# Class tokens' atom products on three column groups, ahead of the patches' first product

## The chip, the cores and the metric

The kernel runs on one core of a Trainium2 chip. Its time is the device time of one execution, in microseconds; it is given as the median of several runs. TensorE (PE) multiplies, with its weight loads shown as PEld; VectorE (DVE), ScalarE (ACT) and GpSimd (POOL) do the elementwise work; SyncE (SP) issues the transfers from HBM. Each engine executes its own instructions in order.

## What is computed

The program is a network of four layers on 512 tokens of width 768. The change lies in the feed-forward part of the second layer (`L1_ffn`). Of its 512 tokens the first six are class tokens, the others patches:

```python
patch_out = gelu(patch_tokens @ fc1_w.T + fc1_b) @ fc2_w.T + fc2_b          # hidden width 192
gate_logits = einsum('bnd,nrd->bnr', l2norm(cls_tokens), l2norm(gate_pair)) + balance_bias
route_probs = softmax(gate_logits); chosen_route = argmax(route_probs)
hid_all = gelu(einsum('bnd,ahd->bnah', cls_tokens, atom_in_w) + atom_in_b)  # 5 atoms x 192
sh_pair = hid_all[:, arange(6)[:, None], src, :]
route_candidates = einsum('bnrh,nrdh->bnrd', sh_pair, atom_out_w[dst]) + atom_out_b[dst]
cls_out = candidate of the chosen route * its probability
return concatenate([cls_out, patch_out], axis=1)
```

Each class token is a row of 768 numbers. It goes through one product to 5 x 192 = 960 hidden numbers (atom-in), is routed, and goes through a second product from 960 back to 768 (atom-out). All of it is in fp32.

## The kernel before

Tokens lie in four tiles of 128 partitions; `xfT` is the normalized input with features on the partitions, in six chunks of 128. The kernel is written with a framework that decides the order of the instructions on each engine when the program is built: it follows the text of the kernel, but moves instructions ahead where it expects them to be ready earlier. Waits between engines come from the use of tiles.

Around the change stand these steps, with their lines:

- L1600: the last product of the graph layer, into `x`. Behind each tile, `Norm` (L230 to L254) takes statistics on VectorE, the square root on ScalarE (L245), and writes the normalized tile `xf` on ScalarE (L254).
- L274: PE transposes `xf` into PSUM; ScalarE (L205) and VectorE (L207) copy it to `xfT` in turn. The transposes of the first two tiles come before those of the last two.
- L298 and L1625: the patches' first product (`fc1`) and its Gelu, into `hid`.
- L1639 to L1667: the routing of the class tokens, on VectorE with a square root (L1641) and an exponential (L1654) on ScalarE; ends with `coef`, the share of each atom for each destination, and `cb`.
- L1677 and L1678: atom-in, in two halves of 480 columns; six matmuls each, with six tokens as the stationary operand, all into the same PSUM partitions; then the bias. L1679 is the Gelu.
- L1685 and L1687: the hidden rows mixed by `coef` into `hin`; L1692 to L1697 transpose them into `hT` (96 partitions, ten chunks of six tokens) and `cb` into `cbT`.
- L1704 to L1706: atom-out, in two halves of 384 columns; ten matmuls with `hT` and one with `cbT` (the bias) each.
- L308: `token_product`, here the patches' second product (`fc2`), whose results are added to `x` (L318), with the statistics of the next norm behind them.

Two helpers matter. `weights` (L143 to L149) takes the next of three weight buffers in turn (`w_tile`) and issues one transfer on SyncE's queue; a transfer waits until what used the buffer three turns before is done, and what stands behind it in the queue waits too. One of the buffers serves until L1600 as `room` for the edges of the graph layer. `routed` (L358 to L375) is the router of other layers: it puts six matmuls on three groups of 32 columns of the array by writing to PSUM partitions 0 to 31, 32 to 63 and 64 to 95; ScalarE copies the 96 rows, and a matmul with the constant `three` (three stacked identities of eight columns) adds the three groups up. `ready` loads a weight and lets POOL make differences of its quarters (L438 to L441); the next layer's first weight, `L2_gnn_W`, is the next that does so.

Of the kernel before, what the change touches and what calls it, by code (L numbers as in the profile page):

```python
# [10 lines left out]
FP = mybir.dt.float32  # L11
# [3 lines left out]
AF = mybir.ActivationFunctionType  # L15
# [3 lines left out]
P = 128  # L19
N = 512  # L20
D = 768
NT = N // P
KC = D // P
HC = D // 2
# [3 lines left out]
HD = 64  # L28
# [69 lines left out]
def kernel(ctx: ExitStack, tc: tile.TileContext, a: dict, out: bass.AP):  # L98
    nc = tc.nc
    V, S, G, T = nc.vector, nc.scalar, nc.gpsimd, nc.tensor  # L100
# [20 lines left out]
    def w_tile(name="w", held=None):  # L121
        pool, n = turn_ = turns.pop(0)
        (turns if held is None else held).append(turn_)
        return pool.tile([P, KC * D], FP, tag="w" + n, name=name)

    def psum():
        return psp.tile([P, 512], FP, tag="ps", name="ps")
# [7 lines left out]
    def feature_major(name):  # L135
        return big_tile(name)[:, : KC * N].rearrange("p (k n) -> p k n", k=KC)
# [6 lines left out]
    def weights(src, p=P):  # L143

        k, n = src.shape[0] // p, src.shape[1]
        w = w_tile()
        v = w[:, : k * n].rearrange("p (k n) -> p k n", k=k)
        nc.sync.dma_start(v[:p], src.rearrange("(k p) n -> p k n", p=p))
        return v  # L149
# [9 lines left out]
    def spread(src, offset, n, parts=P):  # L159

        return bass.AP(tensor=src.tensor, offset=src.offset + offset, ap=[[0, parts], [1, n]])

    def row_tile(name, n=D):
        return rowp.tile([P, KC * (P + 2)], FP, tag="row", name=name)[:, :n]
# [12 lines left out]
    def col(name, i=0, p=P):  # L177
        c = _COL_AT[name] + i
        return cols[:p, c : c + 1]
# [113 lines left out]
    def feature_product(w, xT, f, width=P):  # L293

        ps = psum()
        n = xT.shape[1]
        for k in range(n):
            T.matmul(ps[:width], w[:, k, f : f + width], xT[:, k, :], start=k == 0, stop=k == n - 1)  # L298
        return ps[:width]
# [47 lines left out]
    G3 = 3 * 32  # L347
    three = const.tile([P, 8], FP, name="three")
# [3 lines left out]
    def router_weights(w_dram, e):  # L352
        w = small.tile([P, KC, 32], FP, tag="rt_w", name="rt_w", bufs=1)
        G.memset(w, 0.0)
        nc.sync.dma_start(w[:, :, :e], w_dram.rearrange("(k p) e -> p k e", p=P))
        return w

    def routed(w, xT, e, use):  # L358

# [535 lines left out]
    with tc.tile_pool(name="gat0", bufs=2) as gp:  # L895
# [46 lines left out]
        for i in range(9):  # L942
# [10 lines left out]
            if i < 8:  # L953
                h, s4, d4 = heads(i) if i else head0
# [183 lines left out]
    xfT, xs, rest = n.T, n.split, n.rest  # L1138
    with tc.tile_pool(name="ffn0", bufs=2) as fp:
# [113 lines left out]
        w2a, w2b = sw[:, KC * 384 : KC * 384 + D], sw[:HD, KC * 384 + D : KC * 384 + 2 * D]  # L1253
# [119 lines left out]
    HW = 96  # L1373
# [240 lines left out]
    with tc.tile_pool(name="ffn1", bufs=1) as fp:  # L1614
        NCLS, NA, H = 6, 5, 192
        C = NCLS
        big1 = token_major("cls1")[:C]
        cls = big1[:, 1, :]
        G.tensor_copy(cls, x[:C, 0, :])
        add_row_to(x, row("f1_b2"))  # L1620
        w1 = weights(a["L1_ffn_fc1_w"])
        hid = feature_major("hid")
        for f, width in ((0, P), (1, HD)):
            ps = feature_product(w1, xfT, f * P, width)
            S.activation(hid[:width, f, :], ps, AF.Gelu, bias=col("f1_b1", f, width))  # L1625


        big2 = token_major("cls2")[:C]
        gpair = big1[:, 2:, :]
        nc.sync.dma_start(gpair, a["L1_ffn_gate_pair"])  # L1630
        bal = fp.tile([C, 2], FP, name="bal")
        nc.sync.dma_start(bal, a["L1_ffn_balance_bias"])
        route = fp.tile([C, 2, NA * NA], FP, name="route")
        nc.sync.dma_start(route, a["route"])
        ss = fp.tile([C, 3], FP, name="ss")
        junk, unit = big2[:, 3, :], big2[:, :3, :]
        rows3 = [xf[:C, 0, :], gpair[:, 0, :], gpair[:, 1, :]]
        for i, v in enumerate(rows3):
            V.scalar_tensor_tensor(junk, v, 1.0, v, op0=ALU.mult, op1=ALU.mult,  # L1639
                                   accum_out=ss[:, i : i + 1])  # L1640
        S.activation(ss, ss, AF.Sqrt)  # L1641
        V.tensor_scalar(ss, ss, 1e-12, None, op0=ALU.max)
        V.reciprocal(ss, ss)
        for i, v in enumerate(rows3):
            V.tensor_scalar(unit[:, i, :], v, ss[:, i : i + 1], None, op0=ALU.mult)
        lo = fp.tile([C, 2], FP, name="lo")
        for i in range(2):
            V.scalar_tensor_tensor(junk, unit[:, 0, :], 1.0, unit[:, i + 1, :], op0=ALU.mult,
                                   op1=ALU.mult, accum_out=lo[:, i : i + 1])
        V.tensor_add(lo, lo, bal)  # L1650
        mx = fp.tile([C, 4], FP, name="mx")
        V.tensor_reduce(mx[:, 0:1], lo, AX.X, ALU.max)
        V.tensor_scalar(lo, lo, mx[:, 0:1], None, op0=ALU.subtract)
        S.activation(lo, lo, AF.Exp)  # L1654
        V.tensor_reduce(mx[:, 1:2], lo, AX.X, ALU.add)
        V.reciprocal(mx[:, 1:2], mx[:, 1:2])
        V.tensor_scalar(lo, lo, mx[:, 1:2], None, op0=ALU.mult)
        V.tensor_tensor(mx[:, 2:3], lo[:, 0:1], lo[:, 1:2], ALU.is_ge)
        V.tensor_tensor(mx[:, 3:4], lo[:, 1:2], lo[:, 0:1], ALU.is_gt)
        V.tensor_mul(lo, lo, mx[:, 2:4])  # L1660

        coef = fp.tile([C, NA, NA], FP, name="coef")
        cf = coef.rearrange("p a s -> p (a s)")
        V.tensor_scalar(cf, route[:, 0, :], lo[:, 0:1], None, op0=ALU.mult)
        V.scalar_tensor_tensor(cf, route[:, 1, :], lo[:, 1:2], cf, op0=ALU.mult, op1=ALU.add)
        cb = fp.tile([C, NA], FP, name="cb")
        V.tensor_reduce(cb, coef, AX.X, ALU.add)  # L1667


        ha = fp.tile([C, NA, H], FP, name="ha")  # L1670
        hf = ha.rearrange("p a h -> p (a h)")
        nc.sync.dma_start(hf, spread(a["L1_ffn_atom_in_b"], 0, NA * H, C))
        for i in range(2):
            w = weights(a["L1_ffn_atom_in_w"][:, ts(i, 480)])
            ps = psum()[:C, :480]
            for k in range(KC):
                T.matmul(ps, xfT[:, k, :C], w[:, k, :], start=k == 0, stop=k == KC - 1)  # L1677
            V.tensor_add(hf[:, ts(i, 480)], hf[:, ts(i, 480)], ps)  # L1678
        S.activation(hf, hf, AF.Gelu)  # L1679
        hin = big2.rearrange("p t d -> p (t d)")[:, : NA * H].rearrange("p (a h) -> p a h", a=NA)  # L1680
        for dst in range(NA):
            for n, s in enumerate(range(3, NA) if dst < 3 else range(3)):
                c1 = coef[:, dst, s : s + 1]
                if n == 0:
                    V.tensor_scalar(hin[:, dst, :], ha[:, s, :], c1, None, op0=ALU.mult)  # L1685
                else:
                    V.scalar_tensor_tensor(hin[:, dst, :], ha[:, s, :], c1, hin[:, dst, :],  # L1687
                                           op0=ALU.mult, op1=ALU.add)
        hT = fp.tile([HW, 2 * NA, C], FP, name="hT")
        ps = psum()[:HW, : 2 * NA * C].rearrange("p (k n) -> p k n", k=2 * NA)  # L1690
        for k in range(2 * NA):
            T.transpose(ps[:, k, :], hin[:, k // 2, ts(k % 2, HW)], ident[:C, :C])  # L1692
        V.tensor_copy(hT, ps)
        cbT = fp.tile([NA, C], FP, name="cbT")
        ps = psum()[:NA, :C]
        T.transpose(ps, cb, ident[:C, :C])
        V.tensor_copy(cbT, ps)  # L1697
        ab = big1[:NA, 0, :]
        nc.sync.dma_start(ab, a["L1_ffn_atom_out_b"])
        wo = [weights(a["L1_ffn_atom_out_w"][i * 480 : (i + 1) * 480, :], HW) for i in range(2)]  # L1700
        for c in range(2):
            ps = psum()[:C, :HC]
            for k in range(2 * NA):
                T.matmul(ps, hT[:, k, :], wo[k // NA][:HW, k % NA, ts(c, HC)], start=k == 0, stop=False)  # L1704
            T.matmul(ps, cbT, ab[:, ts(c, HC)], start=False, stop=True)
            V.tensor_add(cls[:, ts(c, HC)], cls[:, ts(c, HC)], ps)  # L1706


        w2 = weights(a["L1_ffn_fc2_w"], HD)
        w2b = weights(a["L1_ffn_fc2_w"][:P, :])  # L1710

        n2 = Norm(x, "xn", 1e-5)

        def use(t, c, ps):
            add_to_x(t, c, ps)
            if t == 0:
                V.tensor_copy(x[:C, 0, ts(c, HC)], cls[:, ts(c, HC)])
            n2.part(t, c)

        token_product([hid[:, 0, :], hid[:HD, 1, :]],  # L1720
                      lambda k: w2b[:, 0, :] if k == 0 else w2[:HD, 2, :], use)

# [331 lines left out]
```

## Time and profile before

| | |
|---|---|
| median of 3 runs | 3091.04 us (3089.36 to 3091.62) |
| the profiled execution | 3090.54 us, span 3088.8 us |
| PE busy | 3004.2 us, 97% of the span |
| DVE, ACT, POOL busy | 1481.0, 753.1, 1430.7 us |
| mean granted clock of TensorE | 0.993 |
| L298, in the stage of the change | 24 rows, 12.1 us |
| L1677 | 24 rows, 9.8 us, 566 ns each |
| L1704 | 40 rows, 16.0 us, 565 ns each |
| L1705 | 4 rows, 1.6 us |
| L308, in this stage | 32 rows, 13.5 us |

A row of the timeline gives the start in us from the span's start, the length, the engine, the line, the operation with its tiles and shapes and how many instructions are merged, and, in brackets, how long the engine was idle before and what ended that. The chain of waits gives start, length and what. A table of stretches gives, for each stretch, its length, the busy time of each engine with its number of instructions, the granted clock of TensorE, the share of the transfer engines and the GB/s. An fp32 matmul of the kernel is two matmul rows of the trace.

### The profile page before, as it was taken

How to read it: one execution, taken by the hardware profiler on the slowest of the kernel's cores; microseconds unless marked ns; L12 is line 12 of the kernel's file. 1: busy time of each engine (PE TensorE's matmuls, PEld its weight loads, DVE VectorE, ACT ScalarE, POOL GpSimd, SP SyncE). 2: the span in 40 equal slices, each digit the busy share in tenths (PEclk: the TensorE clock that was granted, in tenths of full speed). 3: DMA queues.
4: the chain of work that ended last, by engine and by line, in shares of the span. 5: the costliest groups of instructions: out<-in, count | busy, mean ns of one | idle time of the engine just before them, and what ended most of it. 6: DMA issues, size and time to landing. Idle time of an engine off the chain costs nothing.

```text
span 3088.8 us, 31610 instructions
## 1 busy us (share of the span) xinstructions
PE 3004.2 (97%) x11757; PEld 2006.4 (65%) x11757; DVE 1481.0 (48%) x3416; ACT 753.1 (24%) x1436; POOL 1430.7 (46%) x1532
## 2 busy tenths in 40 slices
PE   7999999999999999999899999999999999999989
PEld 3555555556766767765675367877777776677755
DVE  9855444555255235456766436333333335462341
ACT  7432322251352112004432213100000012221111
POOL 4344444452506553645641434455544457355610
PEclk9999999999999999999999999999999999999999
DMA  3211111222203223322112412122222223122222
GB/s 116 89 63 64 65 64 69 72 92 82 82 1 118 77 87 118 111 75 80 38 72 63 148 67 98 67 92 93 92 92 78 77 92 123 67 83 82 99 75 62
DMA packets 92691, 253.63 MB, mean 82 GB/s; under 512 B 9889, under 2 KB 14881, under 8 KB 91514
## 3 DMA queue, kind: packets, MB, share of 16 engines
q1 hardware_dynamic: 92538, 251.61, 23.5%
q8 instruction: 93, 1.52, 0.2%
q14 instruction: 60, 0.49, 0.1%
HBM read 244.23 MB, written 7.36 MB: 81 GB/s over the span
## 4 chain that ended last, share of the span: by engine, by line
PE 87%; DVE 9%; POOL 2%; ACT 1%; issue 1%; DMA 0%; SPq 0%; POOLq 0%; ACTq 0%; DVEq 0%
PE ps L512 43%; PE ps L605 23%; PE ps L904 5%; PE ps L308 4%; DVE oh L705 1%; PE ps L1112 1%; PE ps L1099 1%; PE ps L298 1%; PE ps L274 1%; PE ps L1937 1%; PE ps L1600 1%; POOL room L1458 1%; DVE edge_w L754 1%; PE ps L708 1%; DVE edge_w L743 1%
## 5 line engine op out<-in xcount | busy, mean ns | idle before, releaser
L438 POOL TENSOR_TENSOR tw<-w 128x384 f32<-128x384 f32 x246 | 247.3, 1015 | 960.0 <-DMA w<-in_L_gnn_W 341.8
L512 PE MATMUL ps<-sx,w 128*128 128x256 f32 x1188 | 317.3, 381 | 2.9 <-DVE sx L420 2.6
L512 PE MATMUL ps<-sx,tw 128*128 128x256 f32 x1188 | 290.3, 381 | 0.4
L605 PE MATMUL ps<-w,sx 128*128 128x384 f32 x720 | 256.5, 487 | 4.2 <-DVE sx L420 2.9
L440 POOL TENSOR_TENSOR tw<-w 128x384 f32<-128x384 f32 x246 | 252.2, 1032 | 9.6
L441 POOL TENSOR_TENSOR tw<-w,tw 128x384 f32<-128x384 f32 x246 | 250.4, 1025 | 10.4
L439 POOL TENSOR_TENSOR w<-w 128x384 f32<-128x384 f32 x246 | 250.8, 1028 | 8.9
L605 PE MATMUL ps<-tw,sx 128*128 128x384 f32 x720 | 250.4, 487 | 0.0
L512 PEld LDWEIGHTS ps<-sx,w 128*128 128x128 f32 x1188 | 225.6, 191 | 37.9 <-PE ps L512 2.2
L512 PEld LDWEIGHTS ps<-sx,tw 128*128 128x128 f32 x1188 | 219.9, 190 | 42.7 <-DVE st_u L551 7.2
L527 ACT COPY st_p<-ps 128x256 f32<-128x256 f32 (+1 forms) x127 | 49.9, 394 | 720.4 <-PE ps L512 681.5
L551 DVE TENSOR_TENSOR st_u<-st_p,ps 128x256 f32<-128x256 f32 (+1 forms) x127 | 57.2, 450 | 338.0 <-PE ps L512 337.9
L605 PEld LDWEIGHTS ps<-tw,sx 128*128 128x128 f32 x720 | 136.3, 190 | 94.6 <-DVE x L1821 1.2
L605 PEld LDWEIGHTS ps<-w,sx 128*128 128x128 f32 x720 | 136.6, 190 | 94.1 <-POOL tw L441 4.1
L654 DVE TENSOR_TENSOR x<-x,ps 128x384 f32<-128x384 f32 x216 | 115.2, 552 | 164.7 <-PE ps L605 163.4
L512 PE MATMUL ps<-xfT,w 128*128 128x256 f32 x720 | 176.9, 380 | 0.2
L512 PE MATMUL ps<-w,sx 128*128 128x384 f32 x456 | 169.2, 492 | 1.8 <-DVE ps L555 1.8
L904 PE MATMUL ps<-edge_wT,h 128*128 128x512 f32 x384 | 166.1, 593 | 0.0
L512 PE MATMUL ps<-tw,sx 128*128 128x384 f32 x456 | 160.4, 488 | 4.7 <-DVE st_u L551 4.2
L554 DVE TENSOR_TENSOR st_u<-st_p,ps 128x256 f32<-128x256 f32 (+1 forms) x127 | 57.2, 450 | 203.2 <-PE ps L512 203.2
L512 PEld LDWEIGHTS ps<-xfT,w 128*128 128x128 f32 x720 | 136.2, 190 | 23.9 <-issue 1.3
L605 PE MATMUL ps<-w,hid 128*128 128x384 f32 x432 | 142.9, 488 | 0.0
(485 smaller groups left out, 5067.6 us busy)
## 6 DMA issues: line engine op xcount, KB each, us to landing
w<-in_L_gnn_W SPq DMA_DIRECT2D x60, 768.0 KB, 6.8
w<-in_L_mix_fc_w SPq DMA_DIRECT2D x48, 768.0 KB, 6.2
row<-in_rows SPq DMA_DIRECT2D x39, 384.0 KB, 4.5
w<-in_L_mix_qkv_w SPq DMA_DIRECT2D x18, 768.0 KB, 5.2
w<-in_L_ffn_w SPq DMA_DIRECT2D x18, 768.0 KB, 7.1
w<-in_L_ffn_routed_gate SPq DMA_DIRECT2D x18, 768.0 KB, 6.0
w<-in_L_ffn_routed_up SPq DMA_DIRECT2D x18, 768.0 KB, 6.6
w<-in_L_ffn_routed_down SPq DMA_DIRECT2D x18, 768.0 KB, 5.7
```

The lines of the kernel that those rows point to most:

```text
L308: T.matmul(ps, parts[k][:, ts(t, P)], w_of(k)[:, ts(c, HC)], start=k == 0, stop=k == n - 1)
L438: G.tensor_sub(tt[:, 0, k], b22[:, k], b12[:, k])
L439: G.tensor_sub(b12[:, k], b12[:, k], b11[:, k])
L440: G.tensor_sub(tt[:, 1, k], b22[:, k], b12[:, k])
L441: G.tensor_sub(tt[:, 2, k], b21[:, k], tt[:, 1, k])
L512: T.matmul(bank, l, r, start=start and k == 0, stop=stop and k == KC // 2 - 1, skip_group_check=True)
L527: S.copy(b["p1"], b["x"])
L551: V.tensor_add(b["u2"], b["p1r"], b["y"])
L554: V.tensor_add(u3, b["p1r"], b["y"])
L605: T.matmul(b[name], l[:, k, ts(m, P)], r[:, k, :], start=start and k == 0, stop=k == KC // 2 - 1, skip_group_check=True)
L654: V.tensor_add(x[:, t, ts(j, HC)], x[:, t, ts(j, HC)], ps)
L904: T.matmul(ps, h[:, s, ts(f, P)], wT[:, s, :], start=s == 0, stop=s == NT - 1)
```

## The change

Five edits, all in this feed-forward part:

1. A new helper `in_groups` puts a list of products on three column groups in turn, copies the 96 rows on ScalarE and returns the copy; a matmul with `three` adds the groups up. Its copy takes a buffer of the pool `row`.
2. Atom-in (both halves, with its bias and its loads) moves from behind the routing to ahead of the patches' first product, and uses `in_groups` with 32 tokens as the stationary operand.
3. The patches' first product and its load move behind the routing and the Gelu of the atoms.
4. Atom-out uses `in_groups`; `hT` and `cbT` get 32 columns, cleared by POOL.
5. The weight of the patches' second product goes into one weight buffer by two transfers (rows 0 to 127, rows 128 to 191), where it took two buffers.

```diff
+    def in_groups(terms, n, name):
+        ps = psum()[:G3, :n]
+        for k, (l, r) in enumerate(terms):
+            T.matmul(ps[ts(k % 3, 32)], l, r, start=k < 3, stop=k + 3 >= len(terms), skip_group_check=True)
+        part = row_tile(name, n)
+        S.copy(part[:G3], ps)
+        return part[:G3]
...
         add_row_to(x, row("f1_b2"))
-        w1 = weights(a["L1_ffn_fc1_w"])
-        hid = feature_major("hid")
-        for f, width in ((0, P), (1, HD)):
-            ps = feature_product(w1, xfT, f * P, width)
-            S.activation(hid[:width, f, :], ps, AF.Gelu, bias=col("f1_b1", f, width))
+        ha = fp.tile([C, NA, H], FP, name="ha")
+        hf = ha.rearrange("p a h -> p (a h)")
+        nc.sync.dma_start(hf, spread(a["L1_ffn_atom_in_b"], 0, NA * H, C))
+        for i in range(2):
+            w = weights(a["L1_ffn_atom_in_w"][:, ts(i, 480)])
+            part = in_groups([(xfT[:, k, :32], w[:, k, :]) for k in range(KC)], 480, "at_p")
+            ps = psum()[:C, :480]
+            T.matmul(ps, three[:G3, :C], part, start=True, stop=True)
+            V.tensor_add(hf[:, ts(i, 480)], hf[:, ts(i, 480)], ps)
...
-        ha = fp.tile([C, NA, H], FP, name="ha")
-        hf = ha.rearrange("p a h -> p (a h)")
-        nc.sync.dma_start(hf, spread(a["L1_ffn_atom_in_b"], 0, NA * H, C))
-        for i in range(2):
-            w = weights(a["L1_ffn_atom_in_w"][:, ts(i, 480)])
-            ps = psum()[:C, :480]
-            for k in range(KC):
-                T.matmul(ps, xfT[:, k, :C], w[:, k, :], start=k == 0, stop=k == KC - 1)
-            V.tensor_add(hf[:, ts(i, 480)], hf[:, ts(i, 480)], ps)
         S.activation(hf, hf, AF.Gelu)
+        w1 = weights(a["L1_ffn_fc1_w"])
+        hid = feature_major("hid")
+        for f, width in ((0, P), (1, HD)):
+            ps = feature_product(w1, xfT, f * P, width)
+            S.activation(hid[:width, f, :], ps, AF.Gelu, bias=col("f1_b1", f, width))
...
-        hT = fp.tile([HW, 2 * NA, C], FP, name="hT")
+        hT = fp.tile([HW, 2 * NA, 32], FP, name="hT")
+        G.memset(hT, 0.0)
...
-        cbT = fp.tile([NA, C], FP, name="cbT")
+        cbT = fp.tile([NA, 32], FP, name="cbT")
+        G.memset(cbT, 0.0)
...
         for c in range(2):
+            terms = [(hT[:, k, :], wo[k // NA][:HW, k % NA, ts(c, HC)]) for k in range(2 * NA)]
+            part = in_groups(terms + [(cbT, ab[:, ts(c, HC)])], HC, "at_p")
             ps = psum()[:C, :HC]
-            for k in range(2 * NA):
-                T.matmul(ps, hT[:, k, :], wo[k // NA][:HW, k % NA, ts(c, HC)], start=k == 0, stop=False)
-            T.matmul(ps, cbT, ab[:, ts(c, HC)], start=False, stop=True)
+            T.matmul(ps, three[:G3, :C], part, start=True, stop=True)
             V.tensor_add(cls[:, ts(c, HC)], cls[:, ts(c, HC)], ps)
-        w2 = weights(a["L1_ffn_fc2_w"], HD)
-        w2b = weights(a["L1_ffn_fc2_w"][:P, :])
+        w2 = w_tile()[:, : 2 * D].rearrange("p (k n) -> p k n", k=2)
+        nc.sync.dma_start(w2[:, 0, :], a["L1_ffn_fc2_w"][:P, :])
+        nc.sync.dma_start(w2[:HD, 1, :], a["L1_ffn_fc2_w"][P:, :])
...
-                      lambda k: w2b[:, 0, :] if k == 0 else w2[:HD, 2, :], use)
+                      lambda k: w2[:, 0, :] if k == 0 else w2[:HD, 1, :], use)
```

More of the change, by code (lines that the diff above doesn't have):

```diff
@@ L1692 @@
             T.transpose(ps[:, k, :], hin[:, k // 2, ts(k % 2, HW)], ident[:C, :C])
-        V.tensor_copy(hT, ps)
-        cbT = fp.tile([NA, C], FP, name="cbT")
+        V.tensor_copy(hT[:, :, :C], ps)
+        cbT = fp.tile([NA, 32], FP, name="cbT")
+        G.memset(cbT, 0.0)
         ps = psum()[:NA, :C]
         T.transpose(ps, cb, ident[:C, :C])
-        V.tensor_copy(cbT, ps)
+        V.tensor_copy(cbT[:, :C], ps)
         ab = big1[:NA, 0, :]
```

## The prediction

> **What bounds the kernel now.** I read the page first: PE is busy 97% of the span at a granted clock of 0.993, and the chain that ended last is 87% PE. So a microsecond is won or lost where PE works or waits in the stage that the change touches. Then I read the chain of waits in order of time through that stage (start, length, what).
>
> ```profile
> 1659.41 20.67 PE ps L1600 x64
> 1680.08 1.32 PE ps L274 x12
> ...
> 1683.52 1.03 ACT xf L254
> ...
> 1684.60 1.19 PE ps L274 x6
> 1685.79 11.85 PE ps L298 x24
> 1697.64 9.77 PE ps L1677 x24
> ...
> 1707.44 0.65 DVE ha L1678
> ...
> 1708.12 1.01 ACT ha L1679
> ...
> 1713.48 9.41 PE ps L1704 x20
> 1722.89 0.74 PE ps L1705 x2
> 1723.62 6.54 PE ps L1704 x20
> 1730.17 0.74 PE ps L1705 x2
> 1730.90 13.45 PE ps L308 x32
> ```
>
> Everything from the end of L1600 (1680.08) to the start of the patches' second product (L308, first row at 1730.83 in the timeline) is one chain of 50.75 us. In it PE streams six-column products (L1677, L1704) at full length, and from 1707.4 to 1713.5 it waits while VectorE and ScalarE make the routed hidden rows. Two rows of the timeline give the prices: the router of the last layer, which already uses three column groups, and its copy.
>
> ```profile
> 2988.24 2.46 PE L365 MATMUL ps<-xfT,rt_w 128*32 128x512 f32 x12
> 2990.74 0.58 ACT L368 COPY rt_p<-ps 96x512 f32<-96x512 f32 x1 [1.99 <-PE ps L365]
> ```
>
> The busy times in stretches of 3.4 us tell about the clock (PE first, PEclk before the DMA share):
>
> ```profile
> 1654.30:1657.70 3.40, 1.88 (x10) 0.90 (x9) 3.30 (x8) 2.40 (x4) 1.52 (x2) 1.00 0.57 147
> 1681.60:1685.00 3.40, 0.85 (x9) 0.61 (x7) 1.71 (x9) 1.52 (x3) 2.50 (x4) 1.00 0.95 344
> 1685.00:1688.40 3.40, 3.40 (x9) 1.73 (x8) 2.89 (x6) 2.35 (x4) 1.59 (x2) 0.50 0.44 141
> 1712.30:1715.70 3.40, 2.58 (x7) 0.74 (x7) 0.70 (x4) 0.00 (x0) 0.00 (x0) 0.50 0.73 141
> ```
>
> After a stretch with 0.85 us of PE work the next ran at half clock; after one with 1.88 us it did not.
>
> **The change part by part.** I take the order in which the changed kernel's instructions stand on each engine, and put durations of the profiled execution into it. A source matmul in fp32 is two rows; on one column group they follow each other by (9.83 − 0.57)/23 = 0.403 us for 480 columns, (6.62 − 0.49)/19 = 0.323 for 384, and an array drain of 0.165 follows (0.568 − 0.403).
>
> *Price of three groups.* Twelve router rows took 2.46 us, where one group would need 11 × 0.43 + 0.59 = 5.3: a factor of 2.16, with some waits for the copies of xfT in it. [...]
>
> *Ahead of the first product.* PE's third and fourth blocks of L1467 now have two rows of L605 between them; PE idled 0.76 us there for ScalarE (1656.70 to 1657.46). That gains 0.65. The two memsets on POOL's queue stand between the L1458 steps of the same chain: 320 columns cost about 0.37 (192 took 0.26), and L1458 waited 2.25 before, but its memory seems to come free only at 1653.0, so about 0.1 is lost. Net −0.55, range −0.7 to +0.3.
>
> *The transposes and atom-in (clock of the old run, before the −0.55).* 18 transposes are done at 1681.9 as before. On DVE the first L1639 (0.93, with its read 0.98) now stands ahead of the last statistics, so all of the last tile's normalization, and the third VectorE copy of xfT, is 0.98 later: 1683.6 instead of 1682.6. The sixth pair of the first atom product therefore starts at 1683.65 and ends at 1684.6. ScalarE copies (to 1685.2), and only behind that copy stands L254 for the last tile: 1685.2 to 1686.25, where it ended at 1684.55. PE folds (0.80) and does one pair of the second product (0.80 and a drain) meanwhile, so the last six transposes run from 1686.95 to 1687.6. Five pairs on three groups are two rounds, 1.6 + 0.17 with a switch: 1689.5. Copy to 1690.1, fold 0.8 and a switch 0.1: the patches' first product starts at 1691.05 instead of 1685.58. It is 5.5 later; with the router's price instead of counted rounds, 6.5.
>
> *The first product.* It took 12.06 us, of which 1685.0 to 1688.4 at half clock: 1.7 lost. The gaps of PE above are at most 1.2 us, so each 3.4 us stretch has over 2 us of work and I take full clock: 10.35, ends 1701.4. Behind it L1677 (9.8 us) and the wait of 6.1 us are gone from PE.
>
> *The chain on DVE and ScalarE, which must be done by then.* Second fold lands 1691.2, bias add 0.64 to 1691.85; from L1643 to the end of L1653 it is 4.34 (1694.81 to 1699.15): 1696.2; exponential 0.25; L1655 to L1667 1.74: 1698.25. ScalarE's Gelu of the atoms, now with its table load, is done by 1693.0, its exp table by 1694.3: hidden; of six table loads four are left, none on the path. The patches' Gelu now follows the exponential: its second half can end at 1702.3, ahead of the copies at atom-out and of L308. L1685 to the start of L1704 was 4.33: hT is ready at 1702.6, 1.1 after the first product's end. Both legs are close; had this leg no cover, it would set the end alone.
>
> *Atom-out.* Before: 17.35 us (1713.48 to 1730.83), of which 1713.48 to 1719.2 at half clock, 2.86 lost. Now per half: ten pairs on three groups, four rounds of 0.645 = 2.58; the bias pair with its switch and drain 0.90 (rows followed by 0.416 and 0.411 at that switch); copy with two hand-overs 0.58; fold 0.645: 4.7. Twice and a switch: 9.5. [...] L308 starts at 1712.2.
>
> *Transfers.* SP's queue: the atom weights now take the two early places, fc1's weight that of the buffer freed by L1600 at 1680.1 (the second atom weight stands behind two small loads that went out at 1653.0, and is in 20 us before its use); 1440 KB took 6.7 us there, so 576 KB are in by 1686.9, needed at 1691.05 (4 us cover). The gate pair, behind it, goes out at 1680.6 as before. Atom-out weights: buffers free at 1684.6 and 1689.5, landed by 1691.5 and 1696.5, needed at 1702.6. fc2's weight in one buffer waits for fc1's last row (1701.4); 384 KB took 3.1 us, so 576 KB are in by about 1707, needed at 1712.2; before, its second part landed at 1730.11 for a use at 1730.83. gnn_W goes out when the first atom-out buffer is free (about 1709), subtracted on POOL by 1714 + 12.8 = 1727; its first use is 24.5 after L308's start (1755.32 − 1730.83), 1736.7. Behind this point the order is the same on all engines, but for POOL's x additions standing between Wk's subtractions.
>
> *Sum.* 1730.83 − 1712.2 = 18.6, and 0.55: 19.2. The profiled execution took 3090.54 (span 3088.8 and 1.7 around it): 3071.3. The median of the runs is 0.5 above it: **3072**. With the larger prices (1.0 for the router's price before fc1, 0.9 at atom-out, 0.85 at L605) it is 3074.8, with the smaller (0.7 and 0.15) 3071.
>
> **The rivals.** *The clock.* [...] So I go by the trace: a stretch with less than some 1.4 us of work (1418.8 to 1422.2 had 1.40 and kept full clock). Atom-out's two copies and the wait for hT leave more than 2 us in each. If it drops all the same, a stretch costs 1.7, and recovery took two stretches at 1712.3: 3074 to 3077.
>
> *The two legs.* If an ungated wait on ScalarE (the copies stand ahead of L254 and of the square root) costs 1 to 2 us more at each of three places, the chain ends later by 3 to 6: 3075 to 3078. For it speaks that the order is serial there; against it that every row in it is measured.
>
> *The groups do not run at once.* Atom-in would take 5.0 each (+2 × 2.7), atom-out 7.1 instead of 3.4 (+7.4): the gain shrinks to 6.4, 3085. The router's 2.46 speaks against it; only the width of 480 and 96 rows are new.
>
> *Slower.* POOL: x additions for tiles 1 to 3 now stand behind Wk subtractions, which wait for Wk's transfer; L1741 needs those additions (first at 1777.6 before, about 1758 after). Wk goes out once the second atom-out buffer is free (1711.7), behind gnn_W, in by about 1726. Landing beyond 1758 costs 1 for 1; it makes the kernel slower than before only from 19 us beyond that. Nothing in the profile is that late.
>
> **How the numbers follow.** Forecast 0.68 (3068 to 3076 for it alone), clock 0.11, legs 0.10, no overlap 0.05, slower 0.03, better than 3068 0.03. From 3067 to 3080 the first three are held. A difference under 0.2% (6 us) is what a measurement of this kernel hardly tells from none. Faster takes forecast, clock, legs, better and a little of no overlap: 0.93; same the rest of it, 0.04; slower 0.03.
>
> **What would show it.** Twelve atom-in rows within 1.8 to 2.5 us; last L254 about 1.2 later against the old run; L298 at 1690.5 and 10.4 long at clock 1.00; hT's copy just before 1702.1; L308 at 1711.6; no 0.5 clock between 1680 and 1725. The forecast is wrong if rows of different groups follow each other by 0.4 instead of about 0.13, if PE waits for a weight at L298 or L308, or if the stage after L308 grows.

## The result, and the profile after

The changed kernel took 3074.80 us by the median of four runs (3072.46 to 3080.17), the kernel before 3091.01 beside it: a ratio of 0.9952, 95% interval 0.994 to 0.9964. Ten more runs of it gave 3072.86 (3070.41 to 3089.17; ratio 0.9953, 0.994 to 0.9965). Forecast were 3072, with 3067 to 3080 as the range.

The profiled execution, however, is the slowest of the four, 3080.17. Its chain of waits through the stage (start, length, what) shows that most of the stage went as worked out, and where it did not:

```profile
1660.03 20.67 PE ps L1610 x64
1680.70 1.97 PE ps L274 x18
1682.67 2.62 PE ps L363 x12
...
1685.32 0.56 ACT at_p L365
...
1685.92 0.97 PE ps L1639 x2
1686.89 0.81 PE ps L363 x2
1687.70 0.81 PE ps L274 x6
1688.51 1.76 PE ps L363 x10
...
1690.95 0.97 PE ps L1639 x2
1691.92 10.64 PE ps L298 x24
1702.56 0.37 PE ps L1704 x6
...
1703.07 0.15 DVE cbT L1710
1703.22 0.34 DVE cls L1698
...
1704.21 5.37 PE ps L363 x22
...
1711.62 5.51 PE ps L363 x20
...
1717.74 0.81 PE ps L1718 x2
1718.55 13.45 PE ps L308 x32
```

From the end of L1610 (1680.70) to L308 (1718.55) are 37.85 us; before, the same two points were 50.82 apart. L363 is the product on column groups (first two places atom-in, last two atom-out), L1639 and L1718 are the folds, L365 their copy. Everything up to 1702.56 lies within a few tenths of the forecast. Then two things are late. The last mixing step (L1698) runs only at 1703.22, behind cbT's copy. And the two atom-out products take 5.4 and 5.5 us, where 3.5 (2.58 and 0.90) were worked out for each. The busy times in stretches of 3.4 us say why (after the length: PE, PEld, DVE, ACT, POOL, then PEclk, the DMA share and GB/s):

```profile
1702.20:1705.60 3.40, 2.49 (x27) 1.36 (x29) 0.70 (x3) 0.68 (x1) 0.00 (x0) 1.00 0.54 172
1705.60:1709.00 3.40, 3.40 (x13) 0.58 (x7) 0.00 (x0) 0.00 (x0) 0.00 (x0) 0.50 0.04 7
1709.00:1712.40 3.40, 2.79 (x13) 0.79 (x13) 0.54 (x1) 0.47 (x1) 0.00 (x0) 0.50 0.00 0
1712.40:1715.80 3.40, 3.40 (x12) 0.93 (x9) 0.00 (x0) 0.00 (x0) 0.00 (x0) 0.50 0.19 22
```

Three stretches of atom-out ran at half clock, 10.2 us in one piece. In all traces here, the changes of the clock inside one execution lie on one grid with 3.413 us between its lines: in the profiles of the kernel before and of the changed kernel all 17 changes of each do, to 4 ns, and the pieces at half clock in the stage of the change last 3.41, 6.83 and 10.24 us. Where the grid lies against the rest of the execution differs: in `bias_96` it lay 0.9 us later against L1610's end than in the changed kernel. I call what lies between two lines a cell. The drop above came behind a cell with 2.49 us of PE work, and the cell at 1705.60, with PE busy for all of its 3.40 us, was followed by another at 0.50.

In the experiments the times are counted from L1610's end, taken as the start of its last row and 0.33 us. On this scale atom-out starts at 33.55 before and at 23.66 after, and L308 at 50.91 and 37.93.

### The profile page after: what moved, and what is told of

Read it like the earlier page. It is cut to its first block, busy times and chain, and to the rows that moved or that the text cites. A ratio compares the mean times of both kernels' runs of the same rounds, so it can differ in the third digit from the quotient of the medians.

```text
span 3078.3 us, 31624 instructions
## 1 busy us (share of the span) xinstructions
PE 2997.9 (97%) x11759; PEld 2003.3 (65%) x11765; DVE 1480.6 (48%) x3416; ACT 752.9 (24%) x1438; POOL 1433.6 (47%) x1534
## 4 chain that ended last, share of the span: by engine, by line
PE 86%; DVE 9%; POOL 2%; ACT 1%; issue 1%; DMA 0%; SPq 0%; POOLq 0%; ACTq 0%; DVEq 0%
PE ps L522 43%; PE ps L615 23%; PE ps L914 5%; PE ps L308 4%; DVE oh L715 1%; PE ps L1122 1%; PE ps L1109 1%; PE ps L298 1%; PE ps L274 1%; PE ps L1951 1%; PE ps L1610 1%; POOL room L1468 1%; DVE edge_w L764 1%; DVE edge_w L753 1%; PE ps L1964 1%
```

## The experiments

**The changed kernel again**, for another profiled execution.

> The changed kernel once more, with another profiled execution. The stretch from the end of the last L1610 row to the first row of L308 was 50.75 us before and 37.8 in the first profile of the changed kernel, where atom-out (L363 rows from hT to L308) took 14.3 us, 10.2 of them at half clock. Theory A (the 3.4 us grid of the clock falls differently in every execution, and the drop at atom-out needs a grid cell that lies on PE's wait for hT): in an execution where it falls otherwise atom-out takes about 9.5 us, the stretch about 33, and the whole about 3072 to 3073. Theory B (rows on three column groups, or the copies between them, always bring the half clock): atom-out takes 14 again, the stretch 37 to 38. Ratio to the kernel before 0.9945 to 0.9955 by both, nearer 0.994 by A.

The second profiled execution (3080.53) had the same cells at half clock (25.0 to 35.2), atom-out 14.27, L308 at 37.93: B's numbers. The other runs speak for A: of the fourteen runs, nine lie between 3070.4 and 3073.8, one at 3075.9, three at 3080.2 to 3080.5 (both profiled ones among them), one at 3089.2. Their mean granted clocks go the same way: 0.993 to 0.997 in the nine, 0.990 to 0.992 in the three, 0.989 in the one. Where in those runs the clock differed is not traced, and in both profiles the grid lay in the same place against L1610's end, to 0.05 us; the cases below that share this part of the code show the other clock.

**Each part alone.** `in_only` keeps atom-out and fc2's two buffers of before, `out_only` keeps the old place and form of atom-in and fc2's two buffers, `w2_only` changes nothing but fc2's buffer.

```diff
 in_only, against the changed kernel:
...
-            part = in_groups(terms + [(cbT, ab[:, ts(c, HC)])], HC, "at_p")
             ps = psum()[:C, :HC]
-            T.matmul(ps, three[:G3, :C], part, start=True, stop=True)
+            for k in range(2 * NA):
+                T.matmul(ps, hT[:, k, :], wo[k // NA][:HW, k % NA, ts(c, HC)], start=k == 0, stop=False)
+            T.matmul(ps, cbT, ab[:, ts(c, HC)], start=False, stop=True)
...
 out_only, against the kernel before: the same lines the other way round
...
 w2_only, against the kernel before:
-        w2 = weights(a["L1_ffn_fc2_w"], HD)
-        w2b = weights(a["L1_ffn_fc2_w"][:P, :])
+        w2 = w_tile()[:, : 2 * D].rearrange("p (k n) -> p k n", k=2)
+        nc.sync.dma_start(w2[:, 0, :], a["L1_ffn_fc2_w"][:P, :])
+        nc.sync.dma_start(w2[:HD, 1, :], a["L1_ffn_fc2_w"][P:, :])
...
```

> Only the atom-in product moved ahead and put on three column groups; atom-out on six columns and fc2's weight in two buffers as before. Theory: the first product ends where it does in the changed kernel, hT is ready 1.6 us behind it, and atom-out costs 14.5 us at full clock or 17.4 with the drop of before: the stretch is 38 to 41 us, 10 to 13 less than before, about 3078 to 3081 us. The L615 rows should stand behind the last L1477 block again, since hT's and cbT's memsets are gone, so the 0.55 us of step one is lost too. Rival (the gain of the change is mostly the groups at atom-out): the stretch stays above 45, 3086 or more.

> Only atom-out on three column groups; atom-in behind the first product as before, fc2's weight in two buffers. Theory: PE still waits about 6 us for hT, so a grid cell without work lies ahead of atom-out and it starts at half clock as it did before; atom-out 17.35 becomes 9.5 (full clock) to 14.3 (half), the stretch 43 to 47.2, and 0.55 from the L605 rows: 3082.5 to 3087. Rival (groups alone bring most of the gain): 3080 or less.

> Only fc2's weight in one buffer, loaded in two pieces behind each other. Theory: before, its last piece landed 0.7 us ahead of its use, so nothing is gained; gnn_W and Wk start earlier and were not waited for: the stretch stays 50.7 us, the time within 1 us of before. Rival (transfers collide: gnn_W's earlier start delays fc2's weight or Wk's subtractions on POOL stand ahead of the x additions): 1 to 3 us slower.

The kernel before beside them: 3089.96 by the median.

| kernel | median (range), us | fc1 from | atom-out from | atom-out takes | L308 at | half clock at atom-out |
|---|---|---|---|---|---|---|
| before | 3089.96 (3088.1 to 3092.1) | 5.65 | 33.55 | 17.36 | 50.91 | 6.8 |
| w2_only | 3089.45 (3088.6 to 3091.5) | 6.00 | 33.43 | 17.15 | 50.58 | 6.8 |
| out_only | 3090.66 (3088.5 to 3091.6) | 5.58 | 33.69 | 15.36 | 49.05 | 13.7 |
| in_only | 3078.31 (3077.8 to 3079.2) | 11.29 | 23.55 | 16.26 | 39.81 | 3.4 |
| changed, profiled | 3080.53 | 11.30 | 23.66 | 14.27 | 37.93 | 10.2 |

`in_only` and `w2_only` came out as expected. `out_only` did not: the groups at atom-out alone won nothing (ratio 1.0002, 0.9992 to 1.0011), because half clock lay over nearly all of atom-out:

```profile
1708.90:1712.30 3.40, 1.00 (x9) 0.68 (x9) 3.21 (x12) 0.15 (x1) 0.00 (x0) 1.00 1.05 218
1712.30:1715.70 3.40, 2.56 (x14) 1.11 (x17) 0.65 (x3) 0.00 (x0) 0.00 (x0) 0.51 0.83 165
1715.70:1719.20 3.50, 3.50 (x12) 0.74 (x7) 0.00 (x0) 0.00 (x0) 0.00 (x0) 0.50 0.00 0
1719.20:1722.60 3.40, 2.83 (x11) 0.62 (x12) 0.31 (x1) 0.47 (x1) 0.00 (x0) 0.50 0.00 0
1722.60:1726.00 3.40, 3.40 (x15) 1.13 (x10) 0.23 (x1) 0.00 (x0) 0.00 (x0) 0.50 0.05 5
```

With the six-column rows of before, the drop ended after two cells, in `in_only` after one. With groups it lasted four here and three in the changed kernel: a product is so short that a cell holds a copy's wait (1719.2 here, 1709.0 in the changed kernel) or the bias pair (1715.7, 1705.6), and the clock stayed down through those. So the parts don't add: in the medians atom-in's part is worth 11.65, atom-out's alone nothing, and what the changed kernel has on top of `in_only` 5.45 (3078.31 less 3072.86): atom-out's groups, with fc2's buffer and the 0.55 us at L605 that comes with hT's memsets.

**The late mixing step.** On VectorE's timeline of the changed kernel, cbT's copy stands ahead of the last mixing step and idles 1.08 us for PE's transpose of cb, which PE reaches only when the first product has ended:

```profile
1703.07 0.15 DVE L1710 COPY cbT<-ps 5x6 f32<-5x6 f32 x1 [1.08 <-PE ps L1709]
1703.15 0.40 DVE L1698 SCALAR_TENSOR_TENSOR cls<-ha,coef,cls 6x192 f32<-6x192 f32 x1
1703.89 0.22 DVE L1705 COPY hT<-ps 96x60 f32<-96x60 f32 x1 [0.35 <-PE ps L1704]
```

```diff
-        V.tensor_copy(cbT[:, :C], ps)
+        S.copy(cbT[:, :C], ps)
```

> The changed kernel, with cbT's copy on ScalarE instead of VectorE. In the changed kernel that copy stands on VectorE ahead of the last mixing step (L1698), and it can't run before PE has transposed cb, which stands behind the first product; so the last mixing step, two transposes and hT's copy start only when the first product has ended: 1.8 us from its end to the first atom-out row. Theory: without the copy on that queue the mixing is done under the first product and atom-out starts 0.8 to 0.9 earlier (22.8 behind L1610's end instead of 23.66). The cell of the clock in which PE waits then has some 0.5 us without rows instead of 1.3; if it is the wait that drops the clock, atom-out runs at full clock in 9.5 us, the stretch is 32.3 instead of 37.9, and the whole about 3071. Rival (the groups' rows or their copies drop the clock): atom-out 14.3 again, the stretch 37.1, 3073 to 3074 by the median. Rival 2 (hT was late for another reason): atom-out starts at 23.6 again.

Atom-out started at 22.97, 0.7 earlier. The clock stayed at 1.00 through it, atom-out took 9.64 and L308 began at 32.61. The whole, 3071 in the expectation, did not follow: the median is 3072.89 (3071.17 to 3075.28; ratio 0.9944, 0.9928 to 0.9961), no different from the changed kernel's ten runs. Of the cell with the wait, the profile says this:

```profile
1701.20:1704.60 3.40, 3.02 (x32) 1.43 (x31) 0.22 (x1) 0.72 (x2) 0.00 (x0) 1.00 0.62 164
```

**Bias on equal rows, and atom-in without groups.**

```diff
 bias_96:
-        cbT = fp.tile([NA, 32], FP, name="cbT")
+        cbT = fp.tile([HW, 32], FP, name="cbT")
...
-        ab = big1[:NA, 0, :]
-        nc.sync.dma_start(ab, a["L1_ffn_atom_out_b"])
+        ab = big0[:HW, 0, :]
+        G.memset(ab, 0.0)
+        nc.sync.dma_start(ab[:NA], a["L1_ffn_atom_out_b"])
...
 plain_in:
-            part = in_groups([(xfT[:, k, :32], w[:, k, :]) for k in range(KC)], 480, "at_p")
             ps = psum()[:C, :480]
-            T.matmul(ps, three[:G3, :C], part, start=True, stop=True)
+            for k in range(KC):
+                T.matmul(ps, xfT[:, k, :C], w[:, k, :], start=k == 0, stop=k == KC - 1)
```

> The changed kernel with cb and its bias on 96 rows (91 of them zeros) instead of 5. Theory: the bias pair waited for the drain of the products only because its rows of the array differ (0.42 at full clock, then 0.35 and its own drain 0.42); with equal rows it runs beside the last pair, and a half of atom-out is 0.75 shorter at full clock, 1.5 at half clock: atom-out 8 us at full clock, 11.5 at half. Rival (a pair on another group always follows in order): no change, 9.5 or 14.3.

> The changed kernel with atom-in ahead of the first product, but on six columns, without groups, copies and folds. Theory: 24 rows at 0.403 and two drains are 10 us, with no copy waited for; the first product starts 12.8 behind L1610's end instead of 11.3, and all behind it is 1.5 later; the order of the atoms ahead of the first product, not the groups, brings most of atom-in's part. Rival (the groups bring the gain): the first product starts 16 or more behind L1610's end.

`bias_96`: atom-out started at 23.66, as in the changed kernel, but at full clock, and took 8.18, 1.46 less than in `cb_act`: the equal rows bring what was expected in the trace (its two runs, 3071.38 and 3074.42, can't tell 1.5 us in the whole). This profile also holds A's point: with the PE instructions of the changed kernel up to hT, but in another place of the grid, the clock did not drop behind the cell with the wait:

```profile
1703.30:1706.70 3.40, 2.51 (x22) 1.23 (x24) 0.69 (x3) 0.21 (x1) 0.00 (x0) 1.00 0.55 178
1706.70:1710.10 3.40, 2.78 (x25) 0.94 (x23) 0.54 (x1) 0.47 (x1) 0.00 (x0) 1.00 0.00 0
```

PE is busy as long in this cell (2.51) as in the changed kernel's (2.49), but not with the same. On the exact lines of the grid, L363 alone, the atom-out products, takes this share (PE's busy time behind the length; first the changed kernel, then `bias_96`):

```profile
1702.18:1705.60 3.42, 1.39 (x15) 1.00 0.53 171
1703.29:1706.71 3.42, 2.26 (x21) 1.00 0.55 177
```

In the changed kernel the first product (L298) adds 0.38, which makes 1.77; nearly all the rest of both cells is transposes that stream six columns. In `bias_96` the grid lay 0.9 us later against L1610's end. Over the fourteen traces, counting only matmuls of more than eight columns, PE worked at most 1.87 us in a full-clock cell that was followed by half clock, and at least 1.42 us in one that was followed by full clock; with all matmuls counted the drops reach up to 2.62. So between 1.42 and 1.87 both occurred, and the small matmuls seem not to count; no run varies them alone.

`plain_in`: the first product started at 13.00, 1.7 later than with groups, atom-out at 24.70, 1.04 later; the median of two runs, 3072.61, can't be told from the changed kernel's. By the trace atom-in's groups are worth about 1 us where atom-out starts; its place ahead of the first product is worth the rest.

**What drops the clock at atom-out.** `out_fill` is `out_only` with six matmuls, whose result nobody reads, in PE's wait for hT.

```diff
+        fill = psum()
+        for k in range(KC):
+            T.matmul(fill, ident, xfT[:, k, :], start=True, stop=True)
         S.activation(hf, hf, AF.Gelu)
...
```

> Only atom-out in groups, as in out_only (atom-out 15.4 us, 13.7 of half clock, nothing won), with six matmuls whose result nobody reads behind the second atom-in product, so that PE works through its wait of 6 us for hT. Theory (it is the wait that drops the clock, and the copies of atom-out that keep it down): no half clock at atom-out, which takes 9.6 us from a start at 33.7 to 34.3 behind L1610's end; L308 starts at 43.3 to 43.9 instead of 49.05, and the whole takes about 3085, 5 less than out_only. Rival (rows on three groups run at half clock whatever lies ahead): 15 us again, 3090.

No half clock at atom-out, which took 9.56; L308 at 43.96 instead of 49.05; median 3084.24 (3082.07 to 3090.69; ratio 0.9986, 0.9977 to 0.9996), 6.4 less than `out_only`. Useless work in the wait made the kernel faster: here it was the wait that dropped the clock (1.00 us of PE work in `out_only`'s stretch from 1708.9, the next at 0.51). Two of the nine runs took 3090.5 and 3090.7. There is no trace of them, but their mean granted clocks are the lowest, 0.992 and 0.991 against 0.993 to 0.995. In the traced run the cell with the rest of the wait (from 1710.5) held 1.75 us of matmuls other than the small ones, which lies in the range where both occurred, so a drop at atom-out would fit.

**What keeps it down.** `out_pair` leaves the wait and issues both products ahead of both folds.

```diff
...
         for c in range(2):
             terms = [(hT[:, k, :], wo[k // NA][:HW, k % NA, ts(c, HC)]) for k in range(2 * NA)]
-            part = in_groups(terms + [(cbT, ab[:, ts(c, HC)])], HC, "at_p")
+            parts.append(in_groups(terms + [(cbT, ab[:, ts(c, HC)])], HC, "at_p"))
+        for c in range(2):
             ps = psum()[:C, :HC]
-            T.matmul(ps, three[:G3, :C], part, start=True, stop=True)
+            T.matmul(ps, three[:G3, :C], parts[c], start=True, stop=True)
```

> Only atom-out in groups, as in out_only, with the wait for hT left as it is, but both products ahead of both folds, so that PE waits for one copy instead of two. Theory (a cell of 3.4 us in which PE waits for a copy keeps the clock at half): the clock drops before the first product as in out_only, but comes back within the two products, after 6.8 us of half clock instead of 13.7; atom-out takes 10.5 to 12 us instead of 15.4, L308 starts at 44.5 to 46 behind L1610's end, 3086 to 3087. Rival (groups of 32 columns don't bring the clock back): 14 us, 3089 or more.

The theory was wrong, and the rival's bound (3089 or more) held for a reason that it does not cover, since L308 uses no groups: 3102.94 (3102.12 to 3103.70), 12 us slower than `out_only`. The half clock lasted 47.8 us, fourteen cells, through atom-out and the whole of L308, which took 25.2 us instead of 13.45. Except for the first cell there was no wait in it:

```profile
1714.10:1717.50 3.40, 3.40 (x15) 0.81 (x10) 0.00 (x0) 0.00 (x0) 0.00 (x0) 0.50 0.00 0
1717.50:1720.90 3.40, 3.40 (x14) 0.76 (x15) 0.00 (x0) 0.47 (x1) 0.00 (x0) 0.50 0.00 0
...
1755.10:1758.50 3.40, 3.40 (x10) 2.19 (x9) 1.93 (x11) 1.86 (x4) 0.00 (x0) 0.50 0.95 294
```

PE's timeline of the same stretch shows what these cells hold: each of them at atom-out has a bias pair on 5 rows of the array next to products on 96, and where they change the next matmul starts 0.13 us later than within a product (0.77 behind the last one instead of 0.64), which I call the drain. Behind them L308 alternates between 128 and 64 rows, and the clock came back (at 1758.5) only at the end of the first cell that held transposes and the next product alone, on 128 rows throughout.

```profile
1712.03 5.30 PE L363 MATMUL ps<-w,hT 96*32 96x384 f32 x20 [0.36 <-issue]
1717.26 1.48 PE L363 MATMUL ps<-cls,cbT 5*32 5x384 f32 x2
1718.67 5.33 PE L363 MATMUL ps<-w,hT 96*32 96x384 f32 x20
1723.93 1.48 PE L363 MATMUL ps<-cls,cbT 5*32 5x384 f32 x2
```

So the last run took the change of rows away, and nothing else (the edit of `bias_96` in `out_pair`).

> out_pair with cb and its bias on 96 rows (91 of them zeros) instead of 5. In out_pair the half clock did not end at atom-out but went on through all of L308, 47.8 us in one piece, though PE had a row under way all the time but for gaps of 0.13 us; each cell of 3.4 us held a change of the active rows (96 and 5 in atom-out, 128 and 64 in L308). In the changed kernel the one cell of atom-out without such a change was the last at half clock. Theory: with equal rows atom-out's two products (8 rounds of 1.29 us at half clock) hold a whole cell without change; the clock comes back in it, after 6.8 us of half clock, atom-out takes about 10, L308 starts at 43.5 to 44.5 behind L1610's end, and the whole takes 3084 to 3086. Rival (rows on three groups don't bring the clock back, whatever their height): half clock through L308 again, 3101 to 3103.

The theory's numbers came: 6.8 us of half clock, atom-out 10.13, L308 at 43.94, 3083.35 (3081.85 to 3085.03; ratio 0.9978, 0.9968 to 0.9988), 19.6 us less than `out_pair`. (L308 waited 0.47 us for its weight here, which is within the 10.13.)

```profile
1710.90:1714.30 3.40, 2.70 (x14) 1.11 (x17) 0.50 (x2) 0.00 (x0) 0.00 (x0) 0.50 0.79 146
1714.30:1717.70 3.40, 3.40 (x21) 1.12 (x17) 0.00 (x0) 0.41 (x1) 0.00 (x0) 0.50 0.00 0
1717.70:1721.10 3.40, 3.40 (x24) 1.09 (x18) 0.22 (x1) 0.54 (x2) 0.00 (x0) 0.99 0.29 82
```

The bias pair on 5 rows decided whether the clock came back before L308: all four runs of `out_pair` took 3102 to 3104, all ten of this one 3081.9 to 3085.0. Whether by its row count or by the drain around it is not told apart by this. The other traces agree. Of all half-clock cells with at least 3.0 us of PE work, the 15 with a change of rows (12 of them in `out_pair`) were all followed by another at half clock; of 104 without a change 95 were the last at half clock, and the nine others, all in the last stage, held nothing but matmuls of eight columns.

**A version without the waits.** `better3` puts both atom-in products ahead of both folds, lets atom-out's folds stand between the first rows of L308, moves cbT's copy and puts the bias on 96 rows. `better4` also takes the patches' first Gelu out of the exponential's way.

```diff
 better3 (the core):
+            parts.append(in_groups([(xfT[:, k, :32], w[:, k, :]) for k in range(KC)], 480, part))
...
+        zero = fp.tile([C, 1], FP, name="zero")
+        V.tensor_scalar(zero, ss[:, 2:3], 0.0, None, op0=ALU.mult)
+        S.activation(ss, ss, AF.Sqrt)
+        for i in range(2):
+            ps = psum()[:C, :480]
+            T.matmul(ps, three[:G3, :C], parts[i], start=True, stop=True)
+            V.scalar_tensor_tensor(hf[:, ts(i, 480)], ps, zero, hf[:, ts(i, 480)],
+                                   op0=ALU.add, op1=ALU.add)
...
             if t == 0:
-                V.tensor_copy(x[:C, 0, ts(c, HC)], cls[:, ts(c, HC)])
+                ps = psum()[:C, :HC]
+                T.matmul(ps, three[:G3, :C], parts[c], start=True, stop=True)
+                V.tensor_add(x[:C, 0, ts(c, HC)], cls[:, ts(c, HC)], ps)
 better4, on top:
-        for f, width in ((0, P), (1, HD)):
-            ps = feature_product(w1, xfT, f * P, width)
-            S.activation(hid[:width, f, :], ps, AF.Gelu, bias=col("f1_b1", f, width))
+        first = psum()
+        for k in range(KC - 1):
+            T.matmul(first, w1[:, k, :P], xfT[:, k, :], start=k == 0, stop=False)
+        ps = feature_product(w1, xfT, P, HD)
+        T.matmul(first, w1[:, KC - 1, :P], xfT[:, KC - 1, :], start=False, stop=True)
```

> The changed kernel with its waits filled: both atom-in products ahead of both folds, the folds behind the last transposes; third square sum ahead of the ha additions; cbT's copy on ScalarE; both atom-out products ahead of their folds, which stand between the first rows of L308; cb and its bias on 96 rows (zeros) instead of 5, so that this pair can run beside the last one of the product. Theory: the first product starts 9.8 to 10 behind L1610's end (11.3 in the changed kernel), atom-out 22.3 (23.66), its two products take 5.5 at full clock, and L308 starts at 28 with two folds of 0.8 still to do: 4 us less than the changed kernel at full clock, 8.5 less than it at half clock: 3066 to 3069. If clock cells with copy waits keep the clock down, there are none left, so at most one half-clock cell (1.7 us). Rival (VectorE's chain sets the end, not PE): atom-out starts no earlier than 23, 3070 to 3071.

> better3 with the first product's last pair of its first half moved behind its second half, so that both of the patches' Gelus stand behind the exponential on ScalarE. In better3 the exponential waited 2 us there (Gelu of the first half, then a table load), and atom-out started 3.1 us behind the first product's end. Theory: the exponential runs 1.9 us earlier, hT is ready 1.2 us behind the first product, atom-out starts 21.4 to 21.6 behind L1610's end (23.34 in better3), L308 at 26.8: 1.8 less, about 3068.4 by the median. Rival (the chain on VectorE has another wait of that size): 22.5 or later, no more than 0.8 less.

`better3`: first product from 9.65, atom-out from 23.34 (not 22.3: the exponential waited 2 us on ScalarE), L308 at 28.62; 3070.24 (3068.47 to 3077.01; ratio 0.9938, 0.9923 to 0.9953), the rival's numbers. `better4`: atom-out from 21.54, L308 at 26.83, both as expected; 3068.62 (3067.24 to 3069.42; ratio 0.9931, 0.9915 to 0.9948). It is 4.2 us below the median of the changed kernel's ten runs, and none of its four runs is as long as the shortest of those; the kernel before ran at 3089.90 beside the one and at 3089.96 beside the other. Its chain of waits has, where the changed kernel waits for copies, products and folds behind each other (L1661 and L1741 are the folds, L1696 to L1698 the first product, L364 the products on groups):

```profile
1686.33 0.97 PE ps L1661 x2
1687.30 4.49 PE ps L1696 x10
1691.79 5.29 PE ps L298 x12
1697.08 1.06 PE ps L1698 x2
...
1699.11 5.35 PE ps L364 x44
1704.46 1.68 PE ps L308 x4
1706.14 0.74 PE ps L1741 x2
```

## Why the prediction was right, and where not

The points "in the clock of the old run" are compared with the profiled execution less 0.62, the difference of the two L1610 ends (1680.70 and 1680.08).

- **L605 between the L1467 blocks, less the memsets: right.** From the end of the last reduction on VectorE (L1443, now L1453) to the first L1600/L1610 row, 6.25 us before and 5.70 after: 0.55 gained, as summed. It is 5.71 in `out_only` and 6.24 in `in_only`: it comes with hT's and cbT's memsets, by way of the changed order.
- **Atom-in and the start of the first product: right.** The fold at 1685.3 (1685.2 forecast for the copy's end), last transposes at 1687.0 (1686.95), second product's end at 1689.6 (1689.5), L298 at 1691.23 (1691.05). The last L254 starts at 1685.15, as worked out (1685.2); the 1.2 that the closing list gave for it should have been 1.7. The twelve rows took 2.68 by the timeline, 0.2 more than the list's upper end; the last pair waited for its copy of xfT. Of the 1.0 that the larger prices add here (a product of 5.0 us on one group takes 2.3 by the router's factor of 2.16, against 1.8 by rounds, and there are two), the 0.2 of L298 is all that showed.
- **The first product: right,** 10.64 instead of 10.35, at clock 1.00. The 0.3 are mostly the longer steps at its first row and where its second half begins.
- **The chain on VectorE and ScalarE: one wait missed.** hT's copy was forecast just before 1702.1 with the 0.55 gained, or 1702.6 without, which is the one to compare on this scale; it ended at 1703.5 (1704.11 less 0.62), 0.9 late. The step took L1685 to L1704 over from before as 4.33 us of work. But before, PE idled and transposed cb at once; now PE reaches that transpose behind the first product, and VectorE's queue has cbT's copy ahead of the last mixing step. A row's length was carried over without asking what it waits for. `cb_act` gives 0.7 of the 0.9 back.
- **Atom-out: 9.5 right at full clock, wrong in the profiled executions.** It took 9.64 in `cb_act` and 9.56 in `out_fill`. At half clock it took 14.27. The step that failed is in the clock rival: "Atom-out's two copies and the wait for hT leave more than 2 us in each" was true by PE's busy time (2.49 us in the cell of the drop), but with the transposes of six columns left out it is 1.77, and that was not enough. The bound of some 1.4 us came from one cell of the old trace; over all traces drops occurred up to 1.87. So where the clock stayed up with the wait as it is, as in the trace of `bias_96`, it was the place of the grid that put enough work into the cell, not the reason given: to this extent the central figure was luck. And "recovery took two stretches" was too few: three here, four in `out_only`, so the rival's price was 4.6 instead of 3.4. Its 3074 to 3077 should have been 3077 and more; with the other differences of the execution it was 3080. Of the prices around the 9.5, the 0.9 in the larger ones is the ten pairs by the router's factor (6.62 / 2.16 = 3.06 a half instead of 2.58); for the 0.7 in the smaller ones no run shows a factor, and full clock gave 0.06 to 0.14 more than the 9.5, not less. ScalarE's copies, counted with their hand-overs as 0.58 at atom-out, took 0.59 there (1709.59 to 1710.18), 0.48 of it the copy of 384 columns; those of 480 took 0.56.
- **Transfers: right,** none was waited for at L298 or L308 in the changed kernel; and behind L308's start the stage is unchanged (24.5 us to the row at 1742.97, 24.5 before).
- **The sum.** With full clock at atom-out L308 would start at 23.66 + 9.64 = 33.3, so 17.6 us earlier than before; with 0.55 that is 18.2, where 19.2 was forecast, and the execution would take 3090.5 − 18.2 = 3072.3, by the forecast's own step 3072.8 for the median. The ten runs' median is 3072.86. In the profiled execution 4.6 go to the half clock at atom-out, 1.2 to cells ahead of the stage (the reduction ended at 1654.16, before at 1652.99), and 1.9 come behind L308's start, nearly all of it in the last stages, where 17.1 us of half clock (2975.4 to 2995.8) stand against 10.2: 3080.2.
- **The rivals.** Groups that don't run at once: no; the rows of three groups start 6 to 7 ns apart, the rounds 0.39 to 0.41 us. The slower case on POOL: no. Longer legs: only the 0.9 above.

Not settled: what a cell must hold to drop the clock between 1.42 and 1.87 us, or to bring it back; and the single run at 3089, of which there is only the clock, 0.989.

## What to carry to other kernels

When a serial product is made short, look at what the same code waited for and did while it was long: here 17 us of slow rows had brought the clock back behind two cells (6.8 us), and the short ones took four (13.7 us), so the gain of one part hung on another part's removing most of the wait ahead of it. Order first, packing second: moving the small products ahead of the big one gave nearly all of the 11.65 us, the groups 1 us there by the trace of `plain_in`. And where a copy that depends on PE stands ahead of other work on its engine, as cbT's on VectorE (1.08 us idle), ask which PE instruction is ahead of that one in the new order.

## What the runs showed of the hardware

- With a pair on 5 rows of the array between products on 96 (`out_pair`) half clock lasted through both products, and 128 and 64 rows in turn (L308) did not end it either, although PE had no wait behind the first cell: 47.8 us in one piece, fourteen cells, against 6.8 us, two cells, when the pair had 96 rows (`out_pair96`; 3102.9 and 3083.4 us).
- Full clock was lost after a cell with 2.49 us of PE work out of 3.4, of which 1.77 were products (the changed kernel), and kept after one with 2.51, of which 2.26 were (`bias_96`). Executions of the changed kernel took 3072 or 3080 us; that the place of the grid decides between them fits this and the granted clocks, but the short ones are not traced.
- A half-clock cell full of matmuls of eight columns was never the last at half clock (nine of nine; one of them from 2985.6 in the changed kernel).
- Work that nobody reads, put into a wait, made `out_only` 6.4 us faster (3090.66 and 3084.24 us).
- With equal row counts the bias pair runs beside the last pair of the product on another column group: atom-out took 8.18 us in `bias_96` against 9.64 in `cb_act`, where it has 5 rows beside 96, both at full clock.
